# Attention of an image block: exponentials of two steps summed by one VectorE instruction, normalized x kept in DRAM

## The chip, the core and the metric

The kernel runs on one core of one Trainium2 chip. The metric is the device time of one launch in microseconds, a median over runs. The core has a matrix engine (TensorE, PE in the profile, with its weight loads as PEld), a vector engine (VectorE, DVE), an engine for functions such as the exponential (ScalarE, ACT), a general one (GpSimd, POOL) and a queue that issues transfers (SyncE, SP). Each engine works through its own instructions in order and waits for others by semaphores. SBUF is the working memory of 128 partitions, PSUM holds the results of matmuls in eight banks, DRAM is the memory off the core.

## What is computed

Two layers act on x of shape (2, 96, 96, 96). The first (a selective scan and a feed-forward part) is not touched by the change. The second layer is, for each of the two images:

```python
x = x + _L1_conv_ref(_ln_c(x), kv_w, q_w, lepe_w, lepe_b, proj_w, proj_b)
t = _to_tokens(x)
t = t + _L1_ffn_ref(_ln_t(t), W1, b1, W2, b2)
x = _from_tokens(t, x)
```

and in `_L1_conv_ref`, with 3 heads of 32 channels, R = 2, N = 9216 tokens and 48 x 48 = 2304 cells of 2 x 2 tokens:

```python
k, v = jnp.split(kv, 2, axis=2)
x_samp = x.reshape(B, C, hh, R, ww, R).mean(axis=(3, 5))
q_samp = jnp.einsum('oc,bchw->bohw', q_w, x_samp).reshape(B, heads, HEAD_DIM, nn_)
lepe = depthwise 5 x 5 convolution of v, plus lepe_b
attn = jnp.einsum('bhdn,bhdm->bhnm', k, q_samp) * scale
attn = jax.nn.softmax(attn, axis=-2)
distribution = jnp.einsum('bhdn,bhnm->bhdm', v, attn).reshape(B, C, hh, ww)
dmat = softmax over the 3 x 3 cells around of (x_unfold . samp_unfold) * dist_scale
feature = jnp.einsum('bnpk,bckn->bnpc', dmat, feat_unfold)
out = proj_w . (feature + lepe) + proj_b
```

So each of the 2304 cells asks all 9216 tokens, and the softmax over the tokens needs, for each head and cell, the sum of 9216 exponentials. The normalized x is needed twice: before the attention for k, q, v and the cells' means, and after it, row by row, for v again (for `lepe`) and for `dmat`.

## The kernel before, in words

The second layer runs three stages for each image, one after the other: `_l1_before`, `_l1_attention` and `_l1_rows`. The first and the last are handed to a planner (`_Plan`): each operation is put down with its engine, an estimated cost and the tiles it reads and writes; the planner lays out an order by these estimates, and `_in_order` (L1720) pins that order on all engines, SP's queue among them. A tile of a pool has a number of buffers, and an operation that needs a new one waits until one is free.

**Before** (`_l1_before`, L1096). The image is worked in 16 stripes of 6 rows (T = 576 tokens). A stripe is loaded from DRAM (L1108, three buffers), normalized over the channels in two halves (L1113 to L1122) into `xn`, which holds the whole image in SBUF (96 x 9216 numbers, 36 KB a partition); k is made from it (L1125, L1128), the cells' means `xs` (L1142 to L1147), v (`values`, L1157) and q (`queries`, L1170). `shared` (L1186) copies the k of the first quarter of the tokens to a fourth strip of partitions.

**Attention** (`_l1_attention`, L1443). A flag is computed from bounds on k and q and read by all engines (L1462); the branch that runs here is `_l1_packed` (L1324). The 72 blocks of 128 tokens are split: the last 54 blocks are taken by the three heads in 54 steps side by side, in partition strips 0 to 2, and the first 18 blocks (SHARED) are done in strip 3, for head 0 in steps 0 to 17, head 1 in 18 to 35 and head 2 in 36 to 53 (`p` is the head, `t` the step within it). So four strips work in each step. The cells go in chunks of 480 (10 rows of cells), five chunks an image, the last with 384.

A step `j` of a chunk `m` consists of:

- `scores` (L1344): four matmuls of k against q into two PSUM tiles of two banks each (`two`, tag `s`, three buffers), two strips to a tile, and one exponential for each tile (L1356) into the tile `pr` (L1346, three buffers, one for each step);
- four matmuls of the exponentials with v (L1413), which accumulate in one of two PSUM banks over the chunk;
- the denominators: VectorE adds `pr` into `sums` (L1426), a tile of four strips of 480 columns. The first step copies (L1421). Where strip 3 changes head, the three heads are added (L1423) and strip 3 is copied (L1424), and at the end of a head's 18 steps strip 3 is added to the head (L1428).

The scores of step j + 1 are issued before the matmuls of step j. TensorE's order is that of the program (L1440).

At the end of a chunk, `close` (L1361) copies the accumulated values away (L1366). Its later parts are woven into the next chunk: at step 2 one matmul with ones for each head adds the denominators over the partitions (L1369), and VectorE inverts them (L1373); at step 6 five matmuls add the parts of strip 3 to the heads' values (L1377, L1381), and VectorE multiplies (L1385). ScalarE puts the parts of strip 3 aside in `av3` at steps 17 and 35 (L1430). The q for strip 3 comes by DMA (`load`, L1342).

**Rows** (`_l1_rows`, L1491). Eight stripes of 12 rows: v again from `xn` with two rows on either side (L1520), the 3 x 3 cells around (`near`, L1544 to L1570), the 5 x 5 convolution by 20 taps on VectorE (L1582, L1585) and 5 on TensorE (L1601), projection, feed-forward part, and the store. For each stripe, `near` uses three blocks of 384 tokens of `xn` (`toks`).

Of the kernel before, what the change touches and what calls it, by code (L numbers as in the profile page):

```python
# [8 lines left out]
F32 = mybir.dt.float32  # L9
# [16 lines left out]
C = 96  # L26
# [1069 lines left out]
def _l1_before(k, P, S, W, M, x2d):  # L1096
# [7 lines left out]
    xn, xs, kH, qH, vT, mk, mq = map(held, ("xn", "xs", "kH", "qH", "vT", "mk", "mq"))  # L1104

    def stripe(s):
        xt, sq = (S.tile(P.wk, [C, T], n, 3, name="n" + n) for n in ("xt", "sq"))
        S.op("sp", 1.0, lambda: nc.sync.dma_start(xt.ap, x2d[:, s * T : (s + 1) * T]), (), (xt,))  # L1108
        here = lambda c: slice(s * T + c * H2, s * T + (c + 1) * H2)

        def norm(c):
            pc, va, rs = ps("nxc"), ps("nva"), S.tile(P.wk, [C, H2], "rs", 4)
            op("pe", H2, lambda: nc.tensor.matmul(  # L1113
                pc.ap[:C, :H2], k.less_mean, xt.ap[:, cols(c)], start=True, stop=True),
                (xt,), (pc,))
            op("act", H2, lambda: nc.scalar.activation(
                sq.ap[:, cols(c)], pc.ap[:C, :H2], AF.Square), (pc,), ((sq, c),))
# [12 lines left out]

        for c in range(2):
            norm(c)
        for n, f in enumerate((ALU.max, ALU.min)):
            op("dve", T, lambda n=n, f=f: nc.vector.tensor_reduce(
                mk.ap[:, n, s : s + 1], kH.ap[:C, s * T : (s + 1) * T], AX.X, f),
                ((kH, s),), ((mk, (n, s)),))
        hs = S.tile(P.wk, [C, WIN, CELLS], "hs", 2)
        cells = lambda: xs.ap[:, 1 + 3 * s : 4 + 3 * s, 1 : CELLS + 1]

        def pairs():  # L1140
            v = xn.ap[:, s * T : (s + 1) * T].rearrange("p (i w t) -> p i w t", w=CELLS, t=2)
# [182 lines left out]
def _l1_packed(k, tc, wk, ps, pa, M):  # L1324

    nc = k.nc
    qH, kH, vT, dist = M.qH, M.kH, M.vT, M.dist  # L1330
    steps = NTOK // 128 - SHARED
# [4 lines left out]
    q3 = {}  # L1336

    def load(m, p):
        if m < len(chunks):
# [3 lines left out]

    def scores(m, j):  # L1344
        n, (p, t) = chunks[m][1] * CELLS, divmod(j, SHARED)
        pr = wk.tile([128, 4, 480], F32, tag="pr", name="pr", bufs=3)  # L1346
        two = [ps.tile([128, 2, 512], F32, tag="s", name="sc", bufs=3) for _ in range(2)]
        for s in range(4):
            rows = slice(s * HD, (s + 1) * HD)
            k0 = (SHARED + j) * 128 if s < HEADS else (p * SHARED + t) * 128  # L1350
            q = qH[rows, cells(m)] if s < HEADS else q3[m, p][rows, :n]
            nc.tensor.matmul(  # L1352
                two[s // 2][:, s % 2, :n], kH[rows, k0 : k0 + 128], q, start=True, stop=True
            )
        for i in range(2):
            nc.scalar.activation(  # L1356
                pr[:, 2 * i : 2 * i + 2, :n], two[i][:, :, :n], AF.Exp, scale=HD**-0.5
            )
        return pr

    def close(m, av, sums, av3):  # L1361

        n = chunks[m][1] * CELLS
        avs = wk.tile([128, 480], F32, tag="avs", name="avs", bufs=2)
        rden = wk.tile([C, 480], F32, tag="rden", name="rden", bufs=1)
        nc.scalar.copy(avs[:, :n], av[:, :n])  # L1366
        yield
        for hd in range(HEADS):
            nc.tensor.matmul(  # L1369
                av[hd * HD : (hd + 1) * HD, :n], k.ones[:, :HD], sums[:, hd, :n],  # L1370
                start=True, stop=True,
            )
        nc.vector.reciprocal(rden[:, :n], av[:C, :n])  # L1373
        yield
        for hd in range(HEADS):
            rows = slice(hd * HD, (hd + 1) * HD)
            nc.tensor.matmul(  # L1377
                av[rows, :n], k.join[:, rows], avs[:, :n], start=True, stop=hd == HEADS - 1
            )
            if hd < HEADS - 1:  # L1380
                nc.tensor.matmul(  # L1381
                    av[rows, :n], k.ident[last, last], av3[last, hd, :n], start=False, stop=True
                )
        r0, rows = chunks[m]
        nc.vector.tensor_tensor(  # L1385
            dist[:, 1 + r0 : 1 + r0 + rows, 1 : CELLS + 1],
            av[:C, :n].rearrange("p (r w) -> p r w", w=CELLS),
            rden[:, :n].rearrange("p (r w) -> p r w", w=CELLS),
            ALU.mult,
        )  # L1390
        yield
# [4 lines left out]
    ahead, rest = scores(0, 0), None  # L1396
    for m in range(len(chunks)):
        n = chunks[m][1] * CELLS
        sums = wk.tile([128, 4, 480], F32, tag="sums", name="sums", bufs=2)
        av3 = wk.tile([128, 2, 480], F32, tag="av3", name="av3", bufs=2)  # L1400
        for j in range(steps):
            p, t = divmod(j, SHARED)
            pr = ahead
# [5 lines left out]
            for s in range(4):  # L1409
# [3 lines left out]
                nc.tensor.matmul(  # L1413
                    (main if s < HEADS else other)[s * HD : (s + 1) * HD, :n],
                    vT[:, blk, hd, :],
                    pr[:, s, :n],
                    start=at == 0,
                    stop=at == end - 1,
                )
            if j == 0:  # L1420
                nc.vector.tensor_copy(sums[:, :, :n], pr[:, :, :n])  # L1421
            elif t == 0:
                nc.vector.tensor_tensor(sums[:, :3, :n], sums[:, :3, :n], pr[:, :3, :n], ALU.add)  # L1423
                nc.vector.tensor_copy(sums[:, 3, :n], pr[:, 3, :n])  # L1424
            else:
                nc.vector.tensor_tensor(sums[:, :, :n], sums[:, :, :n], pr[:, :, :n], ALU.add)  # L1426
            if t == SHARED - 1:
                nc.vector.tensor_tensor(sums[:, p, :n], sums[:, p, :n], sums[:, 3, :n], ALU.add)  # L1428
                if p < 2:
                    nc.scalar.copy(av3[last, p, :n], other[last, :n])  # L1430
            if t == 1:

                load(m + (p + 2) // 3, (p + 2) % 3) if j > 1 or m else load(0, 2)
            if rest and j in (2, 6):
                next(rest)
        rest = close(m, main, sums, av3)
        next(rest)
# [53 lines left out]
def _l1_rows(k, P, S, W, ffn, M, distT, x2, out, q, at):  # L1491
# [8 lines left out]
    xn, xs = S.held(M.xn, "xn"), S.held(M.xs, "xs")  # L1500


    vch = S.tile(P.wk, [C, R + 4, HW + 4], "vch", 3)
    y0 = q * R - 2

    def edges():
        nc.gpsimd.memset(vch.ap[:, :, 0:2], 0.0)  # L1507
# [8 lines left out]
    def values(g):  # L1516
# [1 line left out]
        n = (hi - lo) * HW  # L1518
        pv = ps("pv2")
        op("pe", n, lambda: nc.tensor.matmul(  # L1520
            pv.ap[:C, :n], W.v, xn.ap[:, lo * HW : hi * HW], start=True, stop=True),
            (xn,), (pv,), (vch,))
        op("act", n, lambda: nc.scalar.copy(
            vch.ap[:, lo - y0 : hi - y0, 2 : HW + 2],
# [9 lines left out]

    def near(i):
        j = 3 * q + i
        toks = slice(j * 384, (j + 1) * 384)
# [145 lines left out]
def _layer1(k, tc, a, x2d, out):  # L1683
    nc = k.nc
    with ExitStack() as st:
# [17 lines left out]
        with tc.tile_pool(name="l1t", bufs=1) as tmp, tc.tile_pool(name="l1p", bufs=1, space=PSUM) as ps:  # L1703
# [6 lines left out]
        img = pool("img", 1)  # L1710

        def plan(st, work):
            P = Ctx()
# [7 lines left out]

        for b in range(NB):
            M = Ctx()
            M.xn = img.tile([C, NTOK], F32, tag="xn", name="xn")
            M.xs = img.tile([C, CELLS + 2, CELLS + 2], F32, tag="xs", name="xs")
            M.dist = img.tile([C, CELLS + 2, CELLS + 2], F32, tag="dist", name="dist")
            nc.gpsimd.memset(M.xs, 0.0)
# [1 line left out]
            with tc.tile_pool(name="kqv", bufs=1) as kqv:  # L1729
# [4 lines left out]
                M.mq = kqv.tile([C, 2, 6], F32, tag="mq", name="mq")  # L1734
                with ExitStack() as st:
                    plan(st, lambda P, S: _l1_before(k, P, S, W, M, x2d[b]))
                _l1_attention(k, tc, M)

            def rows(P, S):
# [111 lines left out]
```

## Time and profile before

The median of three timed runs is 9014.57 us (9014.46 to 9014.84).

| | us |
|---|---|
| median of the timed runs | 9014.57 |
| the profiled execution, its time | 9021.88 |
| its span, first to last instruction | 9020.1 |
| first layer, up to about | 6935 |
| before, image 1 and 2 | 77 and 80 |
| attention, image 1 and 2 | 625 and 626 |
| rows, image 1 and 2 | 338 and 339 |

Stage by stage the engines were busy as follows (us; image 1):

| stage | from to | TensorE | VectorE | ScalarE | GpSimd | DMA share |
|---|---|---|---|---|---|---|
| before | 6935 to 7012 | 69.1 | 41.7 | 59.3 | 29.8 | 0.20 |
| attention | 7012 to 7637 | 616.3 | 580.5 | 485.3 | 0.0 | 0.01 |
| rows | 7637 to 7975 | 298.5 | 288.3 | 219.0 | 121.1 | 0.08 |

How to read such tables: a busy time is the time in which an engine has an instruction under way. Matmuls are pipelined and often show as busy while they only follow another engine, so a busy time near the length of the stage is not yet the limit. The lines of a timeline name the start, the time of a run of equal instructions, the engine, the line of the code, the operation, and what it writes from what. A wait line says which instruction waited for which, for how many microseconds in all, how often, and the longest.

### The profile page before, as it was taken

The numbers are of one execution on the slowest core, as the hardware profiler recorded it, in microseconds if no ns is written. First come the engines' busy times: TensorE is split into PE (matmuls) and PEld (weight loads), VectorE is DVE, ScalarE is ACT, GpSimd is POOL, SyncE is SP. The second block draws the span as 40 slices with busy tenths as digits, with TensorE's granted clock in tenths as the row PEclk, the third lists the DMA queues.
The fourth block names the chain that finished last, engine by engine and source line by source line (L and its number), as shares of the span: only waits on it lengthen the run. The fifth ranks groups of instructions, "written<-read, shape, count | busy, mean of one in ns | idle before, by whom it ended". The sixth has DMA issues, their size and how long they took to land.

```text
span 9020.1 us, 122080 instructions
## 1 busy us (share of the span) xinstructions
PE 7473.2 (83%) x43537; PEld 3552.9 (39%) x43537; DVE 8098.6 (90%) x5663; ACT 6393.2 (71%) x10720; POOL 6194.7 (69%) x3931
## 2 busy tenths in 40 slices
PE   6888788888878887888788888878866999989998
PEld 3343334444434443344344444334423333543345
DVE  2999999999999999999999999999996898969988
ACT  4677777777777777777777777777754777677867
POOL 3988888888888888888888888898874000320013
PEclk9889888988888888888898989888866999999999
DMA  2444444444444444444444444444442000010000
GB/s 75 138 140 142 140 139 145 140 141 141 135 140 139 135 147 140 141 142 139 144 140 137 142 136 141 137 140 139 138 140 68 3 3 4 21 30 2 3 9 24
DMA packets 335679, 969.58 MB, mean 107 GB/s; under 512 B 50424, under 2 KB 52144, under 8 KB 334768
## 3 DMA queue, kind: packets, MB, share of 16 engines
q1 hardware_dynamic: 335056, 961.64, 33.7%
q8 instruction: 346, 5.67, 0.3%
q14 instruction: 277, 2.27, 0.1%
HBM read 788.04 MB, written 132.17 MB: 102 GB/s over the span
## 4 chain that ended last, share of the span: by engine, by line
DVE 39%; PE 14%; issue 3%; ACT 2%; POOL 1%; DVEq 1%; DMA 0%; SPq 0%; POOLq 0%; ACTq 0%
DVE h L1021 19%; DVE bp L1011 11%; DVE sums L1426 6%; PE sc L1352 4%; DVE acc L1585 3%; PE av L1413 3%; PE y L1034 1%; PE pp L1601 1%; PE pd L669 0%; PE nxc L1113 0%; POOL e L1550 0%; DVEq L1021 0%; PE pk L1125 0%; PE px L608 0%; PE pv L1157 0%
## 5 line engine op out<-in xcount | busy, mean ns | idle before, releaser
L1024 POOL TENSOR_TENSOR h<-h,cre 128x864 f32<-128x864 f32 x2048 | 4122.8, 2021 | 826.7 <-DVE h L1021 415.0
L1021 DVE TENSOR_TENSOR_SCAN h<-dA,bp 128x864 f32<-128x864 f32 x2048 | 4001.5, 1954 | 252.3 <-PE y L1034 6.4
L997 ACT ACTIVATE dA<-dlr,A 128x576 f32<-128x576 f32 x3072 | 2157.0, 765 | 1219.5 <-DVE h L1021 1127.9
L1011 DVE TENSOR_TENSOR bp<-dur,B 128x864 f32<-128x864 f32 x2048 | 2175.8, 1062 | 257.2 <-DMA dur<-du_d 45.5
L1034 PE MATMUL y<-h,fold 128*32 128x288 f32 (+2 forms) x18432 | 1877.9, 454 | 106.3 <-POOL h L1024 102.2
L1008 PE MATMUL B<-bt,selb 128*128 128x288 bf16 x2048 | 637.6, 313 | 1095.3 <-DVE bp L1011 1087.5
L536 PE MATMUL pc<-xin,off 96*96 96x288 f32 x4608 | 1325.0, 414 | 0.9 <-ACT xin L501 0.9
L1034 PEld LDWEIGHTS y<-h,fold 128*32 128x32 f32 x18432 | 766.0, 119 | 1359.0 <-issue 623.2
L1356 ACT ACTIVATE pr<-sc 128x960 f32<-128x960 f32 (+1 forms) x1080 | 955.4, 937 | 258.0 <-DVE sums L1426 146.1
L1426 DVE TENSOR_TENSOR sums<-sums,pr 128x1920 f32<-128x1920 f32 (+1 forms) x510 | 1059.2, 2077 | 60.2 <-ACT pr L1356 7.0
L536 PEld LDWEIGHTS pc<-xin,off 96*96 96x96 f32 x4608 | 708.0, 164 | 622.8 <-issue 379.9
L1507 POOL MEMSET vch<- 96x32 f32 x16 | 2.0, 125 | 1312.8 <-DVE dist L1385 1269.0
L1352 PE MATMUL sc<-qH,kH 32*128 32x480 f32 (+1 forms) x3240 | 710.2, 602 | 9.8 <-DMA q<-qH 9.8
L1352 PE MATMUL sc<-q,kH 32*128 32x480 f32 (+1 forms) x1080 | 564.3, 602 | 0.0
L1413 PE MATMUL av<-pr,vT 128*32 128x480 f32 (+1 forms) x4320 | 532.9, 564 | 3.8 <-ACT av L1430 3.5
L1585 DVE SCALAR_TENSOR_TENSOR acc<-vch,lepe_w,acc 96x1152 f32<-96x1152 f32 x304 | 489.9, 1612 | 7.6
L1008 PEld LDWEIGHTS <-selb 128*128 128x128 bf16 x2048 | 201.9, 100 | 710.5 <-issue 634.5
L1352 PEld LDWEIGHTS sc<-qH,kH 32*128 32x128 f32 x3240 | 285.0, 184 | 439.6 <-issue 304.3
L709 PE MATMUL pt<-xd,w_dt 96*128 96x288 f32 x768 | 317.5, 506 | 25.9 <-ACT zs L519 13.9
L728 POOL TENSOR_TENSOR e<-e,du 128x576 f32<-128x576 f32 x192 | 271.0, 1412 | 32.2 <-ACT du L724 32.0
L1550 POOL TENSOR_TENSOR e<-e,mask 100x384 f32<-100x384 f32 x96 | 171.5, 1808 | 175.6 <-ACT e L1548 175.3
L730 POOL TENSOR_TENSOR dl<-dl,r 128x576 f32<-128x576 f32 x192 | 270.2, 1407 | 6.2
(260 smaller groups left out, 10182.2 us busy)
## 6 DMA issues: line engine op xcount, KB each, us to landing
cre<-c_d SPq DMA_DIRECT2D x1024, 288.0 KB
dur<-du_d SPq DMA_DIRECT2D x256, 864.0 KB
dlr<-dl_d SPq DMA_DIRECT2D x256, 864.0 KB
x<-xs SPq DMA_DIRECT2D x512, 72.0 KB
du_d<-du SPq DMA_DIRECT2D x128, 288.0 KB
dl_d<-dl SPq DMA_DIRECT2D x128, 288.0 KB
du_d<-du SPq DMA_DIRECT2D x128, 144.0 KB
dl_d<-dl SPq DMA_DIRECT2D x128, 144.0 KB
```

Of the source, the lines that this page charges most:

```text
L536: pe(H2, lambda: nc.tensor.matmul(pc.ap[:C, :H2], k.w_c1[:, ih, tap, oh * C : (oh + 1) * C], xin.ap[:, ih, 3 * c + dy : 3 * c + dy + 3, dx ...
L997: S.op("act", 0.76, lambda blk=blk: nc.scalar.activation(dA.ap[:, :, blk, :], dlr.ap[:, blk, :].rearrange("p (c n) -> p c n", c=2), AF.Exp ...
L1008: S.op("pe", 0.3, lambda: nc.tensor.matmul(pB.ap[:, :H2], k.selb[:, kk, i, :], f.bc[o].ap[:, toks], start=True, stop=True), (f.bc[o],), (p ...
L1011: S.op("dve", 1.13, lambda: nc.vector.tensor_tensor(bp.ap[:, : NBL * H2].rearrange("p (b n) -> p b n", b=NBL), dur.ap[:, :, toks], pB.ap[: ...
L1021: nc.vector.tensor_tensor_scan(hv, dv, bv, 0.0, ALU.mult, ALU.add)
L1024: S.op("pool", 2.06, lambda: nc.gpsimd.tensor_tensor(ht.ap, ht.ap, cre.ap[:, toks].unsqueeze(1).to_broadcast([128, NBL, H2]), ALU.mult), ( ...
L1034: nc.tensor.matmul(dst, k.fold, v, start=False, stop=stop)
L1352: nc.tensor.matmul(two[s // 2][:, s % 2, :n], kH[rows, k0 : k0 + 128], q, start=True, stop=True)
L1356: nc.scalar.activation(pr[:, 2 * i : 2 * i + 2, :n], two[i][:, :, :n], AF.Exp, scale=HD**-0.5)
L1413: nc.tensor.matmul((main if s < HEADS else other)[s * HD : (s + 1) * HD, :n], vT[:, blk, hd, :], pr[:, s, :n], start=at == 0, stop=at == e ...
L1426: nc.vector.tensor_tensor(sums[:, :, :n], sums[:, :, :n], pr[:, :, :n], ALU.add)
L1585: S.op("dve", 1.6, lambda: nc.vector.scalar_tensor_tensor(acc.ap, src(), W.lw[:, t : t + 1], acc.ap, ALU.mult, ALU.add), (vch,), (acc,))
```

## The change

It does three things.

1. Two steps share one tile of exponentials, `[128, 2, 4, 480]`, three of them; VectorE adds it into `sums` after every second step, two steps by one instruction. `sums` keeps both halves apart and has five places in each: 1 to 3 for the heads, and 0 or 4 for strip 3. The order of the strips in the tile alternates with the head p: for p = 0 and 2 strip 3 is put in place 0, for p = 1 in place 3, so that four neighbouring places of `sums` always take the sum. The matmuls and the two exponentials of a step take the order 1, 2, 3, 0 of strips where p is even.
2. The closing adds the parts with ones on TensorE: two matmuls for head 0 and four each for heads 1 and 2, in four rounds, two rounds at step 2 and two at step 4, with the inversion; the joining matmuls and the product come at step 8. On VectorE only one addition of strip 3 to a head is left (head 0). `avs` and `av3` have one buffer.
3. `xn` is a tile of the stage `_l1_before` alone. Each stripe of it is stored to DRAM (`M.xd`); 14 rows for the first stripe of `_l1_rows` are loaded before the attention (`M.xn0`), and each later stripe loads its 16 rows (14 the last one) into one of two buffers.

```diff
@@ _l1_before
+    xn = S.tile(P.wk, [C, NTOK], "xn", 1)
...
+        S.op("sp", 1.0, lambda: nc.sync.dma_start(
+            M.xd[:, s * T : (s + 1) * T], xn.ap[:, s * T : (s + 1) * T]), ((xn, s),), ())
@@ _l1_packed
+    strips = lambda p: (0, 1, 2, 3) if p % 2 else (1, 2, 3, 0)
+    place = lambda s, p: s if p % 2 else (s + 1) % 4
...
-        pr = wk.tile([128, 4, 480], F32, tag="pr", name="pr", bufs=3)
+        if j % 2 == 0:
+            pairs[m, j] = wk.tile([128, 2, 4, 480], F32, tag="pr", name="pr", bufs=3)
+        pr = pairs[m, j - j % 2][:, j % 2]
         two = [ps.tile([128, 2, 512], F32, tag="s", name="sc", bufs=3) for _ in range(2)]
-        for s in range(4):
-            rows = slice(s * HD, (s + 1) * HD)
+        for s in strips(p):
+            rows, to = slice(s * HD, (s + 1) * HD), place(s, p)
...
-                two[s // 2][:, s % 2, :n], kH[rows, k0 : k0 + 128], q, start=True, stop=True
+                two[to // 2][:, to % 2, :n], kH[rows, k0 : k0 + 128], q, start=True, stop=True
             )
-        for i in range(2):
+        for i in (0, 1) if p % 2 else (1, 0):
@@ close
-        avs = wk.tile([128, 480], F32, tag="avs", name="avs", bufs=2)
+        avs = wk.tile([128, 480], F32, tag="avs", name="avs", bufs=1)
...
-        for hd in range(HEADS):
-            nc.tensor.matmul(
-                av[hd * HD : (hd + 1) * HD, :n], k.ones[:, :HD], sums[:, hd, :n],
-                start=True, stop=True,
-            )
+        for r in range(4):
+            for hd in range(HEADS):
+                parts = [sums[:, u, v, :n] for v in ((1,), (2, 4), (3, 0))[hd] for u in range(2)]
+                if r < len(parts):
+                    nc.tensor.matmul(
+                        av[hd * HD : (hd + 1) * HD, :n], k.ones[:, :HD], parts[r],
+                        start=r == 0, stop=r == len(parts) - 1,
+                    )
+            if r == 1:
+                yield
@@ the loop of _l1_packed
-        sums = wk.tile([128, 4, 480], F32, tag="sums", name="sums", bufs=2)
-        av3 = wk.tile([128, 2, 480], F32, tag="av3", name="av3", bufs=2)
+        sums = wk.tile([128, 2, 5, 480], F32, tag="sums", name="sums", bufs=2)
+        av3 = wk.tile([128, 2, 480], F32, tag="av3", name="av3", bufs=1)
...
-            if j == 0:
-                nc.vector.tensor_copy(sums[:, :, :n], pr[:, :, :n])
-            elif t == 0:
-                nc.vector.tensor_tensor(sums[:, :3, :n], sums[:, :3, :n], pr[:, :3, :n], ALU.add)
-                nc.vector.tensor_copy(sums[:, 3, :n], pr[:, 3, :n])
-            else:
-                nc.vector.tensor_tensor(sums[:, :, :n], sums[:, :, :n], pr[:, :, :n], ALU.add)
+            if t % 2:
+                pr = pairs.pop((m, j - 1))
+                at = p % 2
+                if j == 1:
+                    nc.vector.tensor_copy(sums[:, :, :4, :n], pr[:, :, :, :n])
+                elif t == 1:
+                    heads = sums[:, :, 1 : 1 + HEADS, :n]
+                    nc.vector.tensor_tensor(heads, heads, pr[:, :, 1 - at : 4 - at, :n], ALU.add)
+                    nc.vector.tensor_copy(sums[:, :, 4 * at, :n], pr[:, :, 3 * at, :n])
+                else:
+                    both = sums[:, :, at : at + 4, :n]
+                    nc.vector.tensor_tensor(both, both, pr[:, :, :, :n], ALU.add)
             if t == SHARED - 1:
-                nc.vector.tensor_tensor(sums[:, p, :n], sums[:, p, :n], sums[:, 3, :n], ALU.add)
+                if p == 0:
+                    nc.vector.tensor_tensor(
+                        sums[:, :, 1, :n], sums[:, :, 1, :n], sums[:, :, 0, :n], ALU.add
+                    )
...
-            if rest and j in (2, 6):
+            if rest and j in (2, 4, 8):
@@ _l1_rows
+    if q:
+        xn = S.tile(P.wk, [C, R + 4, HW], "xn", 2)
+        S.op("sp", 1.5, lambda: nc.sync.dma_start(
+            xn.ap[:, : min(R + 4, HW - y0)],
+            M.xd.rearrange("p (r w) -> p r w", w=HW)[:, y0 : min(y0 + R + 4, HW)]), (), (xn,))
+    else:
+        xn = S.held(M.xn0, "xn")
@@ _layer1
-            M.xn = img.tile([C, NTOK], F32, tag="xn", name="xn")
+            M.xd = dram.tile([C, NTOK], F32, tag="xd", name="xd")
+            M.xn0 = img.tile([C, 2 * WIN + 4, HW], F32, tag="xn0", name="xn0")
...
+                nc.sync.dma_start(
+                    M.xn0[:, 2:], M.xd[:, : (2 * WIN + 2) * HW].rearrange("p (r w) -> p r w", w=HW))
                 _l1_attention(k, tc, M)
```

More of the change, by code (lines that the diff above doesn't have):

```diff
@@ L1103, in _l1_before @@
     held = lambda name: S.held(getattr(M, name), name)
-    xn, xs, kH, qH, vT, mk, mq = map(held, ("xn", "xs", "kH", "qH", "vT", "mk", "mq"))
+    xs, kH, qH, vT, mk, mq = map(held, ("xs", "kH", "qH", "vT", "mk", "mq"))
+    xn = S.tile(P.wk, [C, NTOK], "xn", 1)
     def stripe(s):
@@ L1335, in _l1_packed @@
     cells = lambda m: slice(chunks[m][0] * CELLS, (chunks[m][0] + chunks[m][1]) * CELLS)
-    q3 = {}
+    q3, pairs = {}, {}
+    strips = lambda p: (0, 1, 2, 3) if p % 2 else (1, 2, 3, 0)
+    place = lambda s, p: s if p % 2 else (s + 1) % 4
     def load(m, p):
@@ L1408, in _l1_packed @@
             main, other = banks[m % 2], banks[(m + p) % 2]
-            for s in range(4):
+            for s in strips(p):
                 blk, hd = (SHARED + j, s) if s < HEADS else (t, p)
@@ L1415, in _l1_packed @@
                     vT[:, blk, hd, :],
-                    pr[:, s, :n],
+                    pr[:, place(s, p), :n],
                     start=at == 0,
@@ L1499, in _l1_rows @@
     temp = lambda name: S.tile(P.wk, [C, T], name, 3)
[L1500 removed]
+    xs = S.held(M.xs, "xs")
     vch = S.tile(P.wk, [C, R + 4, HW + 4], "vch", 3)
     y0 = q * R - 2
+    if q:
[5 more added lines that the diff above has]
+        xn = S.held(M.xn0, "xn")
     def edges():
@@ L1520, in values @@
         op("pe", n, lambda: nc.tensor.matmul(
-            pv.ap[:C, :n], W.v, xn.ap[:, lo * HW : hi * HW], start=True, stop=True),
+            pv.ap[:C, :n], W.v, xn.ap[:, lo - y0 : hi - y0], start=True, stop=True),
             (xn,), (pv,), (vch,))
@@ L1536, in near @@
         j = 3 * q + i
-        toks = slice(j * 384, (j + 1) * 384)
+        toks = slice(4 * j - y0, 4 * j - y0 + 4)
         e = [S.tile(P.wk, [NEAR, 384], "e", 4) for _ in range(2)]
@@ L1709, in _layer1 @@
             nc.vector.tensor_tensor(W.pb, W.pb, pl[:C, 0:1], ALU.add)
-        img = pool("img", 1)
+        img, dram = pool("img", 1), pool("l1d", 1, space=DRAM)
         def plan(st, work):
```

## The prediction

> **What bounds it now.** I read the table of stretches first, because the page's averages (DVE 90%) are mostly the first layer, which the change does not touch. The diff works only after 6935 us of the profile. There each of the two images has three stages: before (77 and 80 us), packed attention (7012 to 7637 and 8055 to 8681, 625 us each), rows (338 us each). Then one period of the attention, from one chunk's first VectorE copy (L1421) to the next one's, and in it the timeline of VectorE and some of TensorE's.
>
> ```profile
> core 0: us, PE busy (x) PEld busy (x) DVE busy (x) ACT busy (x) POOL busy (x), PEclk, DMA share, GB/s
> 7142.20:7268.40 126.20, 125.84 (x884) 38.59 (x880) 120.42 (x62) 100.49 (x112) 0.00 (x0) 1.00 0.01 3
> ...
> 7022.80:7043.20 20.40, 20.40 (x162) 5.56 (x160) 19.46 (x10) 18.21 (x20) 0.00 (x0) 1.00 0.00 1
> ```
>
> ```profile
> 7142.22 1.15 DVE L1421 COPY sums<-pr 128x1920 f32<-128x1920 f32 x1
> 7143.47 6.68 DVE L1426 TENSOR_TENSOR sums<-sums,pr 128x1920 f32<-128x1920 f32 x3
> 7150.07 3.15 DVE L1373 RECIPROCAL rden<-av 96x480 f32<-96x480 f32 x1
> 7153.14 8.88 DVE L1426 TENSOR_TENSOR sums<-sums,pr 128x1920 f32<-128x1920 f32 x4
> 7161.94 0.65 DVE L1385 TENSOR_TENSOR dist<-av,rden 96x480 f32<-96x480 f32 x1
> 7162.50 22.51 DVE L1426 TENSOR_TENSOR sums<-sums,pr 128x1920 f32<-128x1920 f32 x10
> 7185.05 0.66 DVE L1428 TENSOR_TENSOR sums<-sums 128x480 f32<-128x480 f32 x1
> 7185.81 1.66 DVE L1423 TENSOR_TENSOR sums<-sums,pr 128x1440 f32<-128x1440 f32 x1
> 7187.38 0.41 DVE L1424 COPY sums<-pr 128x480 f32<-128x480 f32 x1
> 7187.89 38.36 DVE L1426 TENSOR_TENSOR sums<-sums,pr 128x1920 f32<-128x1920 f32 x17
> ```
>
> VectorE has no hole: each row begins where the last ended, and 61 instructions with 120.42 us of work fill 126.20 us, so each carries about 0.095 us between it and the next. PE shows as busy too, but a busy matmul row is not a limit. The list of waits tells them apart:
>
> ```profile
> ACT pr L1356 <- DVE sums L1426: 73.2, 149, 2.8
> ...
> ACT pr L1356 <- PE sc L1352: 44.2, 74, 8.0
> ```
>
> In the first image ScalarE waits 149 times for a `pr` buffer that VectorE still reads. So the sums set the pace: 2.16 us each and one every 38.36/17 = 2.256 us. How far off is the next limit? The stretch 7022.80 to 7043.20, where VectorE had not yet fallen back by all three buffers, holds ten steps (16 matmul records each): 2.04 us a step, matmuls and exponentials feeding each other. VectorE is only 0.21 us a step slower than this.
>
> **Part 1, fused sums (VectorE).** A sum over 480 columns takes 0.657 us (L1428), over 1920 2.158 us: 1.042 ns a column and 0.157 us fixed. So 3840 columns: 4.16 us, with the gap 4.26 against 4.51 for two. [...] I take the row: 0.25 us a pair.
>
> A 480-column chunk then has 24 pair sums (99.8 us), one copy of 3840 columns (2.15, from 0.403 at 480 and 1.152 at 1920), two head sums of 2880 (3.16 each) with two copies of 960 (0.65 each), one join of 960 (1.16; three of 0.66 before), reciprocal 3.15 and product 0.65: 114.6 us in 33 instructions, with gaps **117.7 us**. Alone this would take 8.5 us off the 126.2.
>
> **Part 2, what TensorE gets.** The denominators took three matmuls a chunk and take ten, in four rounds. Which row prices them?
>
> ```profile
> 7144.56 0.98 PE L1369 MATMUL av<-sums,ones 128*32 128x480 f32 x6
> ...
> 7153.54 0.97 PE L1377 MATMUL av<-avs,join 128*32 128x480 f32 x2
> ...
> 7154.44 0.99 PE L1381 MATMUL av<-av,ident 32*32 32x480 f32 x2
> ...
> 7155.36 0.99 PE L1377 MATMUL av<-avs,join 128*32 128x480 f32 x2
> ```
>
> Each matmul is two records. The three of L1369 run side by side, and the next work starts 0.91 us later; the five of L1377 and L1381 come singly, every 0.92 us. [...] L1377/L1381 alternate 128*32 with 32*32; the new ones are all 128*32 on separate column strips within a round, so I price by L1369: 4 x 0.91 = 3.6 us. Singly it would be 9.2.
>
> TensorE's chunk after: 54 x 2.046 (ten steps, start to start, take 20.46) = 110.5; rounds 3.6; L1377/L1381 4.6; waits for ScalarE's two `av3` copies (L1430: 7.2 us over ten) 1.4. Sum **120.1 us**, above VectorE's 117.7. So the pace changes hands, and of VectorE's 8.5 us only 126.2 - 120.1 = 6.1 come out. This overtaking is my central claim. The buffers can't avert it: three pairs let TensorE run ahead by a pair or two, they don't make it faster.
>
> The added wait: at step 2 TensorE waits for the last pair sum of the previous chunk, with the next scores and all later exponentials queued behind it. If TensorE had its full lead this would cost up to one pair sum (4.2 us). As TensorE sets the pace its lead is small at the boundary, and I take 0; VectorE instead idles about 2 us a chunk there, before the reciprocal or pair 4/5.
>
> **Sum for one image.** Chunk 0 took 130.0 us from the first scores at 7012.2 to 7142.2, with some 7 us of VectorE idle at the start. After: 113.7 of work (no closing) and 10 idle, since the first copy waits for step 1 (7018.3, not 7016.2) and the next for step 3 (7024.5): gain 6.2. Chunks 1 to 3: 6.1 each. Chunk 4 (384 columns) took 104.4; TensorE needs 0.8 x 111.9 + 8.2 = 97.7: gain 6.7. Last closing, which nothing covers: three more rounds at the lowered clock seen there (1.42 us a matmul of L1377): -4.3. Sum 26.9, rounded to **27.5** for the sum L1428 that goes from the end (0.56). Two images: **-55 us**.
>
> **Part 3, order of strips and buffers.** In each step the first two score matmuls now write `two[1]` in two thirds of the steps, and its exponential comes first. If score buffers are given out at first write, this is the present rotation with names exchanged: 0. If they are given out in the order of the list, rival D. `avs` and `av3` with one buffer: written at the end of a chunk and at step 17, last read at step 8: 0. Moving the second call of the closing from step 6 to 4 and 8: within the PE sum.
>
> **Part 4, x in DRAM.** Sixteen stores of 216 KB an image go into SP's queue among the loads. SP already waits 43.7 us there for free `nxt` buffers (13 waits on nxc L1113), so loads come just in time. A store waits for the normalization; whatever load stands behind it waits too. Bounds: below, 0 (the planner puts it after the loads that can go; ScalarE, with 59.6 us busy in 80, sets this stage); above, some 2 us for each of 13 loads, +26. Nearest is the planner's order: +1 an image. The load of 14 rows (504 KB) goes before the attention's branch; last x at 7000.5, flag read at 7007.3, and a 216 KB load took 2.9 us from issue to its matmul: hidden, at most +2 if the branch waits for it. Seven loads of 576 KB in the rows: the first can be issued at 7637.1, and the matmuls that need it came at 7647.8; from 2.9 us for 216 KB I estimate 5 to 8 us, so it is hidden under the 27 us of taps of the first stripe (19 x 1.41). A shifted order of the planner: -4 to +4. Taken together **+2** for both images.
>
> **The number.** Span 9020.1, run 9021.9 in the profile; minus 55 plus 2 gives 8967 and 8969. The median of the timed runs is 9014.57, 7.3 below the profiled run, so **8961 us**.
>
> **Rivals.**
> - B, VectorE keeps the pace (TensorE's closing hides in the lead of two pairs): 117.7 a chunk; gains 6.2 + 3 x 8.5 + 8.8 - 4 = 36.5 an image: 8944. For it: VectorE has no hole today although TensorE pays 5.5 us a chunk for its closing. Against: 120.1 over 117.7. Chance 0.13.
> - C, the ten matmuls run singly: +5.6 a chunk, period 125.7, and the gain is nearly gone: about 9008. For it: L1377. Against: L1369. 0.08.
> - D, slower: score buffers by the order of the list. Then the first matmuls of a step take the buffer whose exponential is the last of the step before. From that exponential's end the matmul half takes 1.12 us and the two exponentials 1.87: 3.0 us a step in 36 of 54 steps, 108 + 37 + some 5 of closing = 150 us a chunk, 720 an image with the small chunk at 0.8, against 576: 2 x 144 us on top of 8961: 9249. It decides as soon as the wait exceeds 0.1 us a step. 0.07.
> - E, stores hold up the loads: above bound, 8961 + 52 = 9013; likelier 8985. 0.06.
> - Forecast: 0.66, own range 8940 to 8980.
>
> The range **8930 to 8992** takes in B and the lower half of E, and leaves out D and C. A measurement here can tell a change of some 0.2% (18 us) from none. Faster 0.84 (forecast, B, most of E, little of C), same 0.08, slower 0.08.
>
> **What would show it.** Pair sums of 4.16 us, about 4.26 apart in VectorE-bound stretches. ScalarE's waits for `sums` much below 73.2 us, with waits for `sc` above them. VectorE holes of some 2 us near each chunk's start. Period 120 us; if it is 118, B; 126, C; 150, D. Rounds 0.91 us each. Stages before and rows within 3 and 5 us of 80 and 338. I am wrong in the main if VectorE still has no hole, or if the two other stages take back more than 10 us an image.

## The result, and the profile after

The changed kernel takes **8957.35 us** (median of 4 runs, 8944.84 to 8960.42), the kernel before 9014.70 beside it: a ratio of 0.9932, 95% interval 0.9917 to 0.9946. The forecast was 8961. The profiled execution has a span of 8958.6 us. These are its stages beside those of the kernel before (us; the borders are the end of the attention's flag, the first scores and the last product `dist`; the 4.4 to 5.1 us between flag and first scores are in no row):

| | before | after | difference |
|---|---|---|---|
| first layer, to the load of `k_w` | 6924.9 | 6919.2 | -5.7 |
| before, image 1, to its flag | 82.3 | 82.5 | +0.2 |
| attention, image 1 | 624.7 | 593.6 | -31.1 |
| rows 1 and before 2 | 414.1 | 417.6 | +3.5 |
| attention, image 2 | 625.1 | 593.8 | -31.3 |
| rows 2 | 339.6 | 342.8 | +3.2 |

So the attention gives 62 us. The first layer's program is the same in both; over the twelve profiles of this study it ended between 6914.4 and 6924.9, so its 5.7 us are no more than this scatter. The other stages are looked at in the first experiment.

One period of the attention after the change, by the table of stretches (a period runs from one chunk's first VectorE copy to the next):

```profile
core 0: us, PE busy (x) PEld busy (x) DVE busy (x) ACT busy (x) POOL busy (x), PEclk, DMA share, GB/s
7129.50:7248.61 119.11, 118.61 (x894) 31.96 (x894) 113.97 (x34) 99.68 (x111) 0.00 (x0) 1.00 0.01 3
```

It was 126.20 us with 120.42 us of VectorE work in 62 rows; now it is 119.11 with 113.97 in 34. VectorE now has some 5 us that it does not work. Its timeline in the first third of this period shows where:

```profile
7129.50 2.15 DVE L1438 COPY sums<-pr 128x3840 f32<-128x3840 f32 x1
7131.76 4.16 DVE L1445 TENSOR_TENSOR sums<-sums,pr 128x3840 f32<-128x3840 f32 x1
7136.32 4.16 DVE L1445 TENSOR_TENSOR sums<-sums,pr 128x3840 f32<-128x3840 f32 x1 [0.41 <-ACT pr L1365]
7140.40 3.15 DVE L1387 RECIPROCAL rden<-av 96x480 f32<-96x480 f32 x1
7143.47 8.36 DVE L1445 TENSOR_TENSOR sums<-sums,pr 128x3840 f32<-128x3840 f32 x2
7151.74 0.65 DVE L1399 TENSOR_TENSOR dist<-av,rden 96x480 f32<-96x480 f32 x1
7154.68 16.95 DVE L1445 TENSOR_TENSOR sums<-sums,pr 128x3840 f32<-128x3840 f32 x4 [2.29 <-ACT pr L1365]
...
7176.76 33.99 DVE L1445 TENSOR_TENSOR sums<-sums,pr 128x3840 f32<-128x3840 f32 x8
```

Two holes, 0.41 and 2.29 us, both with ScalarE's exponentials as releaser; after them VectorE works without one to the next chunk. A pair sum takes 4.16 us, and eight take 33.99: from the first start to the last that is 33.99 - 4.16 us for seven distances, so one starts every 4.26 us. The holes lie where TensorE does the closing of the chunk before:

```profile
7129.64 1.81 PE L1381 MATMUL av<-sums,ones 128*32 128x480 f32 x12 [0.44 <-DVE sums L1445]
7135.36 1.78 PE L1381 MATMUL av<-sums,ones 128*32 128x480 f32 x8
7145.16 0.97 PE L1391 MATMUL av<-avs,join 128*32 128x480 f32 x2
7146.06 0.99 PE L1395 MATMUL av<-av,ident 32*32 32x480 f32 x2
```

Two rounds take 1.8 us each time (ten matmuls, two records each), the joining ones come singly, 0.9 us apart, as before. And the list of waits of the first image's attention has turned round; the row of ScalarE waiting for VectorE's sums, 73.2 us before, is gone from it:

```profile
ACT pr L1365 <- PE sc L1361: 86.3, 172, 7.7
DVE sums L1445 <- ACT pr L1365: 15.9, 10, 3.8
```

ScalarE waits for scores, and VectorE for ScalarE. This is what the forecast's central claim asks for. But VectorE is also gapless over two thirds of a chunk, which by itself would speak for VectorE. The two must be told apart by experiment.

### The profile page after: what moved, and what is told of

Read it like the earlier page. It is cut to its first block, busy times and chain, and to the rows that moved or that the text cites. A ratio compares the mean times of both kernels' runs of the same rounds, so it can differ in the third digit from the quotient of the medians.

```text
span 8958.6 us, 121632 instructions
## 1 busy us (share of the span) xinstructions
PE 7398.0 (83%) x43677; PEld 3483.9 (39%) x43677; DVE 8034.8 (90%) x5373; ACT 6390.4 (71%) x10720; POOL 6184.8 (69%) x3931
## 3 DMA queue, kind: packets, MB, share of 16 engines
q14 instruction: 271, 2.22, 0.1%
## 5 line engine op out<-in xcount | busy, mean ns | idle before, releaser
L1445 DVE TENSOR_TENSOR sums<-sums,pr 128x3840 f32<-128x3840 f32 (+1 forms) x240 | 959.0, 3996 | 54.6 <-ACT pr L1365 32.5
L1361 PE MATMUL sc<-qH,kH 32*128 32x480 f32 (+1 forms) x3240 | 626.7, 601 | 9.6 <-DMA q<-qH 4.9
L1361 PEld LDWEIGHTS sc<-qH,kH 32*128 32x128 f32 x3240 | 219.1, 184 | 418.2 <-issue 219.1
L827 ACT CAST fh<-fph 128x288 f16<-128x288 f32 x384 | 141.7, 391 | 195.3 <-PE fph L824 194.5
```

Source lines behind the costliest of these rows:

```text
L1361: nc.tensor.matmul(two[to // 2][:, to % 2, :n], kH[rows, k0 : k0 + 128], q, start=True, stop=True)
L1445: nc.vector.tensor_tensor(both, both, pr[:, :, :, :n], ALU.add)
```

## Experiments

The kernel before ran on the same chip in between. It took 9016.53 us beside the runs on x in DRAM, less work for VectorE, the joining matmuls and head by head; 9013.02 beside the two instructions, two pair tiles, the order of the strips and the later closing; 9019.0 beside the one half and the last run of all. Times of different groups can thus differ by some 6 us for no reason of the kernel, and the periods in the profiles are the safer comparison.

### x in DRAM alone

The function `_l1_packed` is that of the kernel before, all else that of the changed one.

> The kernel before with the third part of the change alone: normalized x stored to DRAM and loaded again, the attention as before. My theory: the attention keeps its 625 us an image and its period of 126.2 us a chunk; the stages around it take back what they show in the changed kernel's profile, about 3 us an image in the rows and 0 in the stage before, so 9015 to 9021 us against 9014.7. The 5.7 us by which the first layer ended earlier in the changed kernel's profile is chance from one execution to the next and stays at 0 in the mean. Rival 1: this part brings some of the gain (another place of the buffers, the first layer 5 us earlier as a rule): 9004 to 9010. Rival 2: the stores hold up the loads and the changed kernel hides it elsewhere: above 9030.

Measured: 9016.52 against 9016.53 us, ratio 1.0002 (0.9993 to 1.0011). The attention keeps 624.1 and 625.1 us. So the third part brings nothing and costs nothing that a run can tell (-6 to +10 us); its profile shows +2.9 for rows 1 with before 2 and +2.2 for rows 2. Rows 2, the same program in all the kernels with x in DRAM, took from 338.9 to 342.9 us in their profiles, so of the 3.2 us in the second image no more is shown than this scatter. Rows 1 with before 2 took 416.0 to 418.8 us in all eleven profiles with x in DRAM, against 414.1 in the one profile of the kernel before: a cost of 2 to 5 us there is likely, but one profile to compare with does not prove it.

### Less work for VectorE

```diff
-                    both = sums[:, :, at : at + 4, :n]
-                    nc.vector.tensor_tensor(both, both, pr[:, :, :, :n], ALU.add)
+                    both = sums[:, :, at : at + 3, :n]
+                    nc.vector.tensor_tensor(both, both, pr[:, :, :3, :n], ALU.add)
```

> The changed kernel with 21 of the 24 whole pair sums of a chunk taken over three of the four strips only (2880 columns in place of 3840): the sums of one strip are left out, so the output is another. Each such sum takes about 3.16 in place of 4.16 us, so VectorE is relieved of some 21 us a chunk, and nothing else changes. My theory (TensorE sets the pace at 119.1 us a chunk): the period falls only by TensorE's own wait for the last pair sum at step 2, 0.4 us, to about 118.7: 8950 to 8957 us. Rival (VectorE still sets the pace, its holes are only the start of a chunk): the period falls to what TensorE needs without VectorE, 54 steps of 2.04 us and little more, 110.5 to 113 us: 8885 to 8900 us.

Every pair sum leaves out one of its four strips; it was all 24 of a chunk, not 21. Measured: 8943.0 us (8939.23 to 8945.23). The stretch of one period:

```profile
7123.69:7242.81 119.12, 118.76 (x896) 32.06 (x894) 90.16 (x33) 100.35 (x111) 0.00 (x0) 1.00 0.01 3
```

VectorE has 24 us less to do, 90.16 in place of 113.97, and the period is 119.12 in place of 119.11. Where it sums pairs it now waits 0.93 us for each next pair, a pair every 4.09 us: that is twice a step of 2.045 us of the matmuls and exponentials. In the third and the fourth chunk each of the 54 steps, by the starts of the exponentials, is as long as in the changed kernel to within 0.01 us. **VectorE does not set the period of the changed kernel.** The run as a whole is shorter than expected (8950 to 8957), by 4.7 and 4.9 us an image in the attention. VectorE's first copy of the second chunk comes 113.6 us after that of the first, where it was 116.9, since VectorE no longer lags; but ScalarE's exponentials keep their 113.7 us (113.5). The gain lies at the end of the image: in the first one the exponentials of the last chunk take 1.2 us less (one step, the one in which TensorE waits for the sums of the chunk before), TensorE waits 1.85 in place of 2.69 us before its last rounds, and some 2 us are the author's estimate for the granted clock of the last closing. That clock differs from one closing to another: in the changed kernel's profile the four rounds took 4.21 us in the first image (granted clock 0.50 from 7588 to 7590 us) and 2.78 us in the second (1.00).

### TensorE's joining matmuls in another order

```diff
             nc.tensor.matmul(
                 av[rows, :n], k.join[:, rows], avs[:, :n], start=True, stop=hd == HEADS - 1
             )
-            if hd < HEADS - 1:
-                nc.tensor.matmul(
-                    av[rows, :n], k.ident[last, last], av3[last, hd, :n], start=False, stop=True
-                )
+        for hd in range(HEADS - 1):
+            rows = slice(hd * HD, (hd + 1) * HD)
+            nc.tensor.matmul(
+                av[rows, :n], k.ident[last, last], av3[last, hd, :n], start=False, stop=True
+            )
```

> The changed kernel with the five joining matmuls in another order: first the three with avs (128 rows, three column strips), then the two with ident (32 rows). The same work[...]. My theory (TensorE sets the pace; matmuls of one mode on separate strips run side by side): the five take two rounds of 0.91 us, 1.8 in place of 4.58 us, TensorE's chunk is 2.8 us shorter, 116.3 us, and VectorE's own 116.4 to 117.1 us take over: period about 116.8, and 2.8 to 4 us less in each of the two last closings that nothing covers. 8927 to 8935 us. Rival 1 (VectorE sets the pace): only the last closings get shorter, 8950 us. Rival 2 (such matmuls run singly whatever their order): 8957 us.

Measured: 8932.23 us (8927.3 to 8936.23), period 116.72. TensorE's timeline:

```profile
7142.52 0.99 PE L1391 MATMUL av<-avs,join 128*32 128x480 f32 x6
7143.44 0.99 PE L1396 MATMUL av<-av,ident 32*32 32x480 f32 x4
```

The three with `avs` run side by side (0.99 us for all of them), then the two with `ident` (0.99 us): two rounds in place of five singles, with one change of the tile shape, 128*32 to 32*32, in place of four. This shape, as the rows print it, is what the expectations call a mode. The two rounds start 0.92 us apart, and the step with the join in it takes 3.86 in place of 6.62 us, by the starts of the exponentials. Taking 2.76 us from TensorE shortens the chunk by 2.4 us; taking 24 us from VectorE did nothing. Here VectorE's hole of 2.29 us is gone, and over two periods TensorE waits 1.7 us and its weight loads 4.1 us for sums: at 116.7 the two are level.

These two runs decide between VectorE and the closing on TensorE. They do not say what sets the 2.045 us of a plain step: ScalarE's two exponentials, 0.965 us each, fill 1.93 us of it, and no run made them or the matmuls of a step cheaper. "TensorE sets the pace" stands below for this chain of matmuls and exponentials with the closing's matmuls in it.

### The denominators head by head

```diff
-        for r in range(4):
-            for hd in range(HEADS):
+        for hd in range(HEADS):
+            for r in range(4):
...
-            if r == 1:
+            if hd == 1:
                 yield
```

> The changed kernel with the ten matmuls of the denominators issued head after head in place of round after round (six at step 2, four at step 4). My theory: matmuls into the same strip run one after the other and only those of neighbouring heads overlap, so eight to ten of 0.9 us in place of four rounds: +3.7 to +5.5 us on TensorE a chunk, which sets the pace, and as much at 1.4 times in each last closing: period 122.8 to 124.6 us, 9002 to 9025 us. Rival 1 (matmuls of one mode overlap whatever strip they write): 8957 us, the rounds are of no use. Rival 2 (VectorE sets the pace and covers TensorE's closing): the period stays within 1 us of 119.1 although the ten matmuls take 7 us or more.

Measured: 8977.72 us (8969.85 to 8983.37), period 122.33. TensorE's timeline:

```profile
7125.31 3.42 PE L1381 MATMUL av<-sums,ones 128*32 128x480 f32 x12 [0.48 <-DVE sums L1445]
7132.64 3.38 PE L1381 MATMUL av<-sums,ones 128*32 128x480 f32 x8
```

Six matmuls (two of head 0, four of head 1) take 3.4 us and four (head 2) take as long. The ten cost 6.7 us in place of 3.45, and the period grows by just this, 3.2 us. The expected 8 to 10 singles did not come, and the run stays below the 9002 to 9025 us expected: the two of head 0 are hidden wholly beside the four of head 1. Four matmuls of one strip took 3.38 us, 0.84 us each, and in both places the longest chain of one strip made the time.

### Pair sums as two instructions

```diff
-                    both = sums[:, :, at : at + 4, :n]
-                    nc.vector.tensor_tensor(both, both, pr[:, :, :, :n], ALU.add)
+                    for u in range(2):
+                        both = sums[:, u, at : at + 4, :n]
+                        nc.vector.tensor_tensor(both, both, pr[:, u, :, :n], ALU.add)
```

> The changed kernel with each of the 24 pair sums of a chunk taken as two instructions of 1920 columns, one for each step; everything else as changed. My theory: VectorE needs 24 x 0.25 us = 6.0 us a chunk more, 116.3 + 6.0 = 122.3 us, more than TensorE's 119.1, so the pace goes back to VectorE: period 122.3 to 122.8 us, 8987 to 8997 us. The fusing by itself is then worth 3.3 of the 7.1 us a chunk, and the other half comes from the two additions and the halved copies and heads' sums that went from VectorE to TensorE. Rival 1 (nearly all comes from the fusing): period 125 to 126 us, 9010 us. Rival 2 (TensorE sets the pace with room to spare): 119.1 us, 8957 us.

Measured: 8948.86 us (8945.82 to 8952.22), period 119.1. The theory fell: undoing the fusing costs nothing, and the attention is even 3.9 us an image shorter than in the changed kernel. The timeline of VectorE shows why:

```profile
7171.68 3.16 DVE L1441 TENSOR_TENSOR sums<-sums,pr 128x2880 f32<-128x2880 f32 x1 [0.97 <-ACT pr L1365]
7174.75 0.65 DVE L1442 COPY sums<-pr 128x960 f32<-128x960 f32 x1
7175.51 33.19 DVE L1446 TENSOR_TENSOR sums<-sums,pr 128x1920 f32<-128x1920 f32 x16
```

Sixteen sums of 1920 columns in 33.19 us: from start to start 2.07. In the kernel before the same instruction came every 2.26 (17 in 38.36) with the same duration of 2.15 to 2.16. So each now starts 0.09 us before the end of the last, where before it started 0.10 us after it. What differs is that the two halves of `sums` alternate, so no sum reads what the one just before it wrote. VectorE waits in this period for 4.7 us (holes of 1.17, 2.22, 0.97 and 0.31): it needs 114.4 us, less than the 116.4 of the fused form.

### The same with one half

```diff
-                        both = sums[:, u, at : at + 4, :n]
+                        both = sums[:, 0, at : at + 4, :n]
```

> As the run unfused (each pair sum taken as two instructions of 1920 columns), but both add into the same half of sums, so each instruction reads what the one before it wrote; the sum is the same. My new theory, after unfused: what costs is not the number of instructions but that each sum waits for the end of the one before. In unfused the two halves alternate, the wait on VectorE's own count is for the instruction before last, and the next one starts 0.08 us before the end of the last: 2.074 us a sum. With one half it is again 2.255 us a sum as in the kernel before, 24 x 0.36 = 8.7 us a chunk more than unfused's 114.4 of VectorE time: about 123.1, VectorE sets the pace, period 122.8 to 123.6 us, 8987 to 9002 us. Rival (1920 columns simply go as fast as this once the pairs of tiles are there, or VectorE reads the pair's tile faster): 119.1 us, 8949 us as unfused.

Measured: 8999.17 us (8994.59 to 9005.91), period 122.7 to 123.1. VectorE's timeline and, from the waits of two periods, the row that is back:

```profile
7184.13 36.10 DVE L1446 TENSOR_TENSOR sums<-sums,pr 128x1920 f32<-128x1920 f32 x16
```

```profile
ACT pr L1365 <- DVE sums L1446: 7.1, 9, 1.0
```

The same number of instructions of the same size, but sixteen take 36.10 in place of 33.19 us, 2.26 apart. One dependence costs 0.19 us a sum, and VectorE sets the pace again. That settles it: the gap after each sum was the price of the chain, not of the instruction.

### Two pair tiles, and the order of the strips

```diff
-            pairs[m, j] = wk.tile([128, 2, 4, 480], F32, tag="pr", name="pr", bufs=3)
+            pairs[m, j] = wk.tile([128, 2, 4, 480], F32, tag="pr", name="pr", bufs=2)
```

> The changed kernel with two tiles of pairs in place of three. My theory: between the closings VectorE (4.25 us a pair) is slower than TensorE (4.09), and falls back by 0.16 us a pair, some 3.5 us a chunk, which it makes up while TensorE does the closing. Three pairs hold this lag. With two, TensorE and ScalarE wait for each pair sum and the closing is no longer covered: a chunk takes VectorE's 116.4 us and its holes, which grow from 2.7 to 6 or 8 us: period 121 to 125 us, 8975 to 9015 us. Rival (the lead is not needed, TensorE is the only limit): 119.1 us, 8957 us.

Measured: 8985.9 us (8983.56 to 8990.89), period 122.27. The waits from 7010 to 7600 us, in the first image's attention:

```profile
ACT pr L1365 <- PE sc L1361: 58.7, 94, 4.8
ACT pr L1365 <- DVE sums L1445: 36.7, 60, 0.9
DVE sums L1445 <- ACT pr L1365: 29.1, 18, 4.1
```

ScalarE waits for sums again, and VectorE for ScalarE too: 29.1 us where it was 15.9. Each engine is held up in its turn. So the gapless two thirds of the changed kernel are VectorE falling back by 0.17 us a pair and living on the third tile; it catches up in the hole that TensorE's closing leaves.

The other run of this pair gives the strips and exponentials the order of their places:

```diff
-    strips = lambda p: (0, 1, 2, 3) if p % 2 else (1, 2, 3, 0)
+    strips = lambda p: (0, 1, 2, 3) if p % 2 else (3, 0, 1, 2)
...
-        for i in (0, 1) if p % 2 else (1, 0):
+        for i in (0, 1):
```

> The changed kernel with the strips of each step worked in the order of their places (3, 0, 1, 2 where p is even, and the exponentials 0, 1), so that the order of the list of score tiles is also the order of writing. My theory: score buffers are given by first write or the order makes no difference for another reason; the names are exchanged only: 8957 us, period 119.1 within 0.3. Rival (the order of the list gives the buffers, and the changed kernel pays for it in two thirds of its steps): the steps get shorter, the pairs fall below 4.09 us, period below 117, 8935 us or less.

Measured: 8953.14 us (8950.44 to 8957.77), periods of 118.92 to 119.14. The order makes no difference; rival D is out. (The 3.0 us a step that it asked for are not in the changed kernel either, whose steps take 2.045.)

### What helps, together

The grouped joining matmuls with the closing at later steps:

```diff
-            if rest and j in (2, 4, 8):
+            if rest and j in (4, 6, 10):
```

> The changed kernel with the joining matmuls grouped by mode, as in the run before, and the three parts of the closing at steps 4, 6 and 10 in place of 2, 4 and 8. My theory: with the grouping TensorE and VectorE need the same, 116.3 us; TensorE's wait of 0.8 us at step 2 for the last pair sum of the chunk before goes, and VectorE's hole of 0.41 us behind it: period 116.3 to 116.5 in place of 116.72, 8928 to 8932 us, no difference that can be told from the 8932 of the grouping alone. Rival (the waits at the chunk's start are a real limit): period 115.5 or less, 8920 us.

Measured: 8926.33 us (8925.33 to 8932.76), period 116.42. As expected, 0.3 us a chunk, which the run cannot tell from the grouping alone.

With the pair sums as two instructions besides:

> The three things that helped, together: the joining matmuls grouped by mode, the closing at steps 4, 6 and 10, and the pair sums as two instructions into alternating halves. My theory: VectorE needs 114.4 us a chunk, TensorE 116.3 and sets the pace: period 116.3 to 116.4 us, as with the first two alone (116.42); the first and the last chunk of an image get shorter by 4 us together, as in unfused, since VectorE no longer lags there: 8914 to 8922 us. Rival 1 (VectorE's lag at the ends is not it): 8926 us as without the third. Rival 2 (TensorE's 116.3 hides some wait for VectorE): period near 115, 8908 us or less.

Measured: **8916.24 us** (8911.81 to 8921.37), ratio 0.9883 (0.9867 to 0.9900): faster than both kernels, with periods of 116.4 and 574.4 us of attention an image. TensorE sets the pace; VectorE has holes at each change of head. The time is within what was expected.

## Why the prediction was right, step by step

**The pace changes hands to TensorE**: right, with TensorE and ScalarE taken together in the plain steps. The two runs that take work from one engine alone decide it against VectorE: 24 us from VectorE, 0.0 us of period; 2.76 us from TensorE, 2.4 us of period. The profile alone would not have shown it, since VectorE is without a hole most of the time.

**TensorE's chunk, 120.1**: measured 119.1. The rounds took 3.45 (3.6 in the sum), the join 4.6 (4.6), 54 steps at 2.045 are 110.4; all that TensorE does beyond them was 8.7 us, not 9.6. The term that was too large is the rest after rounds and join, put at 1.4 for the `av3` copies; some 0.6 to 0.7 is left for it. The wait at step 2 for the last pair sum, taken as 0, was 0.44 us in the period shown; in the next two the step with these rounds takes the same 3.57 us as in the run with less work for VectorE, so there it was 0; in the last chunk, whose steps are shorter, it was 1.00. VectorE's holes, put at 2 us, are 2.7.

**VectorE's chunk, 117.7**: measured 116.4, the period less its holes. The work of 114.6 us was right (113.97). The gap of 0.095 us on each of 33 instructions was not (the sum lists 32, which changes little): the row gave it for a chain of sums, and in these profiles it shows only where an instruction needs the result of the one before. The copy at 7176.00 of the changed kernel's profile starts 0.08 us before the end of the sum ahead of it, whose result it does not read.

**What fusing is worth, 0.25 us a pair**: right within a chain (4.26 against 2 x 2.26; the prediction's 2.256 divides the row by its 17 sums, not by the 16 distances between them), and it moved the period from 122.9 (one half, two instructions) to 119.1, about half of the 7.1 us; the rest, found by difference and not by a run of its own, goes to the additions, copies and heads' sums that went. But the reason was wrong. The prediction put the 0.25 us down to each instruction, as 0.157 us fixed and a gap of 0.095 us, both estimated from the rows of the kernel before; by that the two-instruction form had to lose. Its 24 extra instructions cost nothing (VectorE needs 114.4 us a chunk, against 116.4 fused), and the removed dependence gave 0.19 us a sum (2.07 against 2.26 from start to start).

**The sum for an image**, forecast 27.5, measured 31.1 in the first:

| term | forecast | measured |
|---|---|---|
| chunk 0 with the start | 6.2 | 6.9 |
| chunks 1 to 3 | 3 x 6.1 | 3 x 7.0 |
| chunk 4 | 6.7 | 5.1 |
| last closing, with L1428 gone | -3.7 | -1.9 |

The last closing was priced by matmuls at the lowered clock, 1.42 us each. Measured, all four rounds took 4.2 us, 2.2 more than the one round of before. The granted clock was lowered for part of them only: in the rows of the trace it is 0.50 from 7588 to 7590 us, 0.86 on the mean from 7590 to 7593 and 0.50 again from 7595, so the first join takes 0.83 us and the next row 1.19 before they come at 1.49. In the second image the four rounds had the full clock (1.00 from 8603 to 8606) and took 2.8 us, and the joins came slowly from the first on (1.49 us each); in the kernel before, the one round was slow from its start (granted clock 0.51). So where in the closing the lowered clock falls is not the same each time: between the two images it made 1.4 us on the rounds and 0.95 us the other way on the joins, and this term was uncertain by as much. In chunk 4, from 7486.86 to 7586.1, TensorE was done after 96.7 us (97.7 in the sum), but the last pair sum still ran on VectorE (2.69 us of TensorE idle before the rounds): the lag that a full chunk makes up in the next one is paid there. Two alternating halves take most of it away (0.58 us idle, and the exponentials of chunk 4 are 1.2 us shorter), which is where most of that form's 3.9 us an image lie.

**x in DRAM, +2**: the profile shows +6.9 over the stages concerned, the timed run of this part alone 0 (-6 to +10). The sign and size stay within what was allowed for; a closer figure is open. (The 2 us a load in the bound for the stores is near what the profile of the kernel before has: a 216 KB load issued at 6986.53 us had its last packet done 2.1 us later.)

**The number, 8961 against 8957.35**, is closer than its parts. The attention gave 62.4 us and not 55; against that the profile has 6.9 us of loss in the other stages and not 2, and the four timed runs alone lie between 8944.84 and 8960.42. A miss of under 4 us is in part luck; the mechanism of the attention is not.

## What to carry to other kernels

A gap between equal instructions may be the price of a dependence, as here, where two halves in turn gave 2.07 us a sum and one half 2.26: before merging them, let two accumulators alternate. When an engine is without holes, take work from it alone and see whether the period moves; here, with three pair tiles of lead, VectorE was gapless for two thirds of the chunk, and 24 us less of its work left the period at 119.12 us. When a merge hands the pace to another engine, look at that engine's cheapest reordering: here five matmuls, put in two groups of one tile shape each (128*32, then 32*32), gave 2.4 us a chunk, a third of what the whole change gave, for no work.

## What the runs showed of the hardware

- A VectorE sum of 1920 columns that reads what the sum before it wrote starts 0.10 us after that one's end; one that doesn't starts 0.09 us before it (2.26 against 2.07 us from start to start, durations of 2.15 to 2.16 both times). In both forms the trace has a record of a wait for VectorE's own semaphore between nearly any two sums. With one half it ends 0.06 us after the end of the sum before, 0.04 us before the next starts; with two it is over 2 us before that end. That this wait makes the difference is the likely reading, and was not tried by itself. The 0.10 us are no constant of a dependence: the addition of strip 3 (L1448 of the changed kernel) reads what the sum before it wrote, has no such record of its own, and starts 0.03 us after it.
- Matmuls on separate column strips overlapped without being neighbours in the program: two of head 0 and four of head 1, issued head by head, took 3.42 us, and four of head 2 alone 3.38 us.
- Two plain steps take 4.09 us (1.96 and 2.13 early in the chunk, by the starts of the exponentials), and stayed so, to 0.01 us, with 24 us of VectorE's work gone. Whether TensorE alone or its exchange with ScalarE sets these 2.045 us a step was not tried.
